# Rows of the quantised FFN's scales by way of DRAM, in pieces of 8 bytes

## The chip, the cores and the metric

The kernel runs on one core of a Trainium2 chip. The metric is device time in microseconds of one execution, lower is better. Before the change three runs took 2035.65, 2041.41 and 2042.34 us, median 2041.41. A core has five engines that run side by side[...]: PE (TensorE, matrix products, with PEld for its weight loads), DVE (VectorE), ACT (ScalarE), POOL (GpSimd) and SP (SyncE, which only issues DMAs here). They wait for one another by semaphores.

## What is computed

Two decoder layers over x of 32 batches x 128 tokens x 256 features: attention, cross-attention and a feed-forward network (FFN) in each. Only the last part, layer 1's FFN, is touched. It quantises its activations twice, once before each product, with one scale per token:

```python
def act_quant(x):
    scale = 127.0 / jnp.clip(jnp.max(jnp.abs(x), axis=-1, keepdims=True), 1e-05)
    return jnp.clip(jnp.round(x * scale), -128, 127) / scale
...
h = bit_linear(x, w1)                       # quantised x, ternary w1: 256 -> 1024
h = depthwise_conv1d(h.transpose(0, 2, 1), conv_w, conv_b)   # 3 taps along the tokens
h = h.transpose(0, 2, 1)
h = jax.nn.silu(h)
return bit_linear(h, w2)                    # quantised h, ternary w2: 1024 -> 256
```

A scale belongs to a token. The kernel has h with features on the 128 partitions and tokens along the free axis, so that the convolution runs along the free axis. To multiply by a token's scale there, a row of 256 token scales must stand on every partition.

## The kernel before

**Stages.** Attention and cross-attention of layer 0 (to about 430 us), layer 0's mixture of experts (to about 1300 us), and `layer1`, which holds the rest. x stays in SBUF throughout, in tiles of four batches.

**Units.** `layer1` splits the 32 batches into NU = 16 units of U = 2 batches, so T = 256 tokens. `unit(u)` returns small functions ("pieces"), one per step: names in d_ are the mixer's, m_ the MLP's, e_ the cross-attention's, f_ the quantised FFN's. The table `PLAN` gives each piece a round, from 0 to 89, and unit u starts STEP = 11 rounds after unit u-1, so some eight units are in work at once. The loop at the end of `layer1` walks the rounds and calls the pieces; that is the program's order.

**Order on the engines.** The products go through `mm` and the transposes through `turned` (L206, L209), which keep PE's instructions in program order. On DVE, ACT, POOL and SP the tile framework orders the instructions itself, from the program's order and its own estimate of when operands are ready. [...] 

**The FFN's steps.** `f_norm` (round 55) normalises x, takes the largest magnitude of each token (`am`, L1259) and calls `scales`, which makes the scale (`qs`, L1010) and its inverse times the weight's mean (`dq`, L1012), both [128 tokens, 2 batches]. `f_quant` scales and rounds (L1265, L1267). `f_flip` (58) transposes the rounded x and calls `on_rows` for dq. `f_h` (60 to 64) makes the first product in four chunks of 256 features and multiplies each by dq's rows (`d`, L1277); `f_z` and `f_taps` are the convolution (L1282, L1292, L1296, L1298), `f_silu` the activation (L1305), `f_top` and `f_am` (67 to 75) the largest magnitude of each token (L1311, L1316, L1323) and its scales. `f_rows` (78) calls `on_rows` for qs; `f_round` (79, 81) multiplies the four chunks of z by qs's rows (L1332) and rounds them (L1333); `f_out` (89) is the second product, its scaling by dq (L1346) and the store (L1349).

**`on_rows` before.** For each of the unit's batches it broadcasts one column of scales along the free axis and multiplies by the identity, so that every partition gets the same row; ACT copies the result from PSUM to SBUF (L1021). It is called twice per unit, once with dq and once with qs.

Other work named later: `m_y`, `m_fc` and `m_out` (tiles y_m, f_m, sT_m, m_m) are the MLP; `e_s`, `e_exp`, `e_soft` and `e_at` (s_e, nm_e, at_e, lv_e) the cross-attention's softmax, with exp on ACT (L1217); `d_v` makes u_d on POOL (L1091); `d_q2` needs a logarithm on ACT (L1097); `d_stats`, `d_nb` (st_d, rs_d, nb_d, ms_d) are the next unit's layer norm. ACT reloads its function table when it changes between exp, logarithm and silu. The loads of `kv_e` and the stores of `out` are layer 1's only other DMAs by SP.

Of the kernel before, what the change touches and what calls it, by code (L numbers as in the profile page):

```python
# [10 lines left out]
F32 = mybir.dt.float32  # L11
# [3 lines left out]
ALU = mybir.AluOpType  # L15
AX = mybir.AxisListType

P = 128
S = 128
# [56 lines left out]
def decoder(ctx: ExitStack, tc: tile.TileContext, a: dict, out: bass.AP):  # L76
    nc = tc.nc
    V, A, PE, GP = nc.vector, nc.scalar, nc.tensor, nc.gpsimd
# [8 lines left out]
    dram = ctx.enter_context(tc.tile_pool(name="scratch", bufs=1, space=bass.MemoryType.DRAM))  # L87
    psp = ctx.enter_context(tc.tile_pool(name="ps", bufs=8, space=bass.MemoryType.PSUM))

    def bank(name, dt=F32):  # L90
        return psp.tile([P, 512 if dt == F32 else 1024], dt, tag="ps", name=name)
# [22 lines left out]
    def con(name):  # L114
        at, w = C_AT[name]
        return cst[:, at : at + w]

    ident, blk, pm = con("ident"), con("blk"), con("pm")
# [86 lines left out]
    def mm(out, lhsT, rhs, start, stop):  # L205
        tc.keep_in_program_order(PE.matmul(out, lhsT=lhsT, rhs=rhs, start=start, stop=stop))  # L206

    def turned(out, in_, by=None):
        tc.keep_in_program_order(PE.transpose(out, in_, ident if by is None else by))  # L209
# [12 lines left out]
    U = 2  # L222
    T = U * S
    NU = NB // U
    ckv = dram.tile([NU, P, 2, U * D], F32, name="ckv")
    rw = keepc.tile([P, 2, NB], F32, name="rw")
    slots = keepc.tile([P, 2, NB], I32, name="slots")
    wm = keepc.tile([P, 2], F32, name="wm")
# [683 lines left out]
    def layer1(wd):  # L912
# [4 lines left out]
        w1 = wq[:, 0, :].rearrange("p (c h) -> p c h", c=2)  # L917
# [3 lines left out]
        with tc.tile_pool(name="pl", bufs=1) as pool, tc.tile_pool(name="pl1", bufs=1) as keep:  # L921
# [10 lines left out]
            def sb(tag, name, bufs=1, dt=F32, shape=(2, T)):  # L932
                return pool.tile([P, *shape], dt, tag=tag, name=name, bufs=bufs)

            def flat(t):
                return t.rearrange("p a b -> p (a b)")

            def bank3(name, n=T):
                return bank(name)[:, : 2 * n].rearrange("p (a b) -> p a b", a=2)

            def sm(tag, name, w=U, bufs=3):
                return small.tile([P, w], F32, tag=f"l_{tag}", name=f"{tag}_{name}", bufs=bufs)
# [34 lines left out]
            def flipped(src, dst, n, dt=F32):  # L977

                pt = bank(f"pt_{n}", dt)[:, : 2 * T]
                for c in range(2):  # L980
                    for i in range(U):
                        turned(
                            pt[:, c * T + i * S : c * T + (i + 1) * S], src[:, i, c * P : (c + 1) * P],
                            ident if dt == F32 else ident_b,
                        )
                A.copy(flat(dst), pt)
                return dst

            def halves(w, m, xT, name):

                p = bank3(name)
                for e in range(2):
                    for c in range(2):
                        mm(p[:, e, :], w[:, c, (m + e) * P : (m + e + 1) * P], xT[:, c, :], c == 0, c == 1)
                return p
# [9 lines left out]
            def scales(am, k, name):  # L1005

                V.tensor_scalar(am, am, 1e-5, None, ALU.max)
                s = sm(f"qs{k}", name)
                V.reciprocal(s, am)
                V.tensor_scalar(s, s, 127.0, None, ALU.mult)  # L1010
                dq = sm(f"dq{k}", name)
                V.tensor_scalar(dq, am, 1.0 / 127.0, wm[:, k : k + 1], ALU.mult, ALU.mult)  # L1012
                return s, dq

            def on_rows(v, k, name):

                p = bank(name)[:, :T]
                for i in range(U):
                    mm(p[:, i * S : (i + 1) * S], v[:, i : i + 1].to_broadcast([P, P]), ident, True, True)
                r = pool.tile([P, T], F32, tag=f"rows{k}", name=f"{name}_sb", bufs=2)  # L1020
                A.copy(r, p)  # L1021
                return r[:, None, :].to_broadcast([P, 2, T])

            def unit(u):
                x = X[u * U // G][:, u * U % G : u * U % G + U, :]
                d_, m_, e_, f_ = f"d{u}", f"m{u}", f"e{u}", f"f{u}"
                o = {}
# [223 lines left out]
                def f_norm():  # L1251
                    o["xf"] = xn = sb("xf", f"xn_{f_}")
                    for i in range(U):
                        V.tensor_scalar(
                            xn[:, i, :], x[:, i, :], o["mv"][:, i, 0:1], o["rs"][:, i : i + 1],
                            ALU.subtract, ALU.mult,
                        )
                    am = sm("am", f_)
                    V.tensor_reduce(am, xn, AX.X, ALU.max, apply_absolute_value=True)  # L1259
                    o["s1"], o["dq1"] = scales(am, 0, f_)  # L1260

                def f_quant():
                    xn = o["xf"]
                    for i in range(U):
                        V.tensor_scalar(xn[:, i, :], xn[:, i, :], o["s1"][:, i : i + 1], MAGIC, ALU.mult, ALU.add)  # L1265
                    o["xi"] = sb("xi", f"xi_{f_}", 2, BF16)
                    V.tensor_scalar(flat(o["xi"]), flat(xn), MAGIC, 127.0, ALU.subtract, ALU.min)  # L1267

                def f_flip():
                    o["hT"] = flipped(o["xi"], sb("xTf", f"xT_{f_}", 2, BF16), f_, BF16)  # L1270
                    o["rows1"] = on_rows(o["dq1"], 1, f"rows1_{f_}")

                def f_h(k):
                    if k == 0:
                        o["z"] = sb("z", f"z_{f_}", 3, shape=(NHC, T))
                    o["d", k] = sb("d", f"d_{f_}_{k}", 4)
                    V.tensor_tensor(o["d", k], halves(w1, 2 * k, o["hT"], f"h_{f_}_{k}"), o["rows1"], ALU.mult)  # L1277

                def f_z(k):
                    for j in range(2):  # L1280
# [37 lines left out]
                def f_am():  # L1318
                    pt = bank3(f"am_{f_}", S)
                    for i in range(U):  # L1320
                        turned(pt[:, i, :], o["top"][:, 0, i * S : (i + 1) * S])
                    am = sm("am2", f_)
                    V.tensor_reduce(am, pt, AX.X, ALU.max)  # L1323
                    o["s2"], o["dq2"] = scales(am, 1, f_)

                def f_rows():
                    o["rows2"] = on_rows(o["s2"], 2, f"rows2_{f_}")
                    o["zi"] = sb("zi", f"zi_{f_}", 2, BF16, (NHC, T))

                def f_round(k):  # L1330
                    z = o["z"][:, 2 * k : 2 * k + 2, :]
                    V.tensor_tensor(z, z, o["rows2"], ALU.mult)  # L1332
                    V.tensor_scalar(  # L1333
                        flat(o["zi"][:, 2 * k : 2 * k + 2, :]), flat(z), MAGIC, MAGIC, ALU.add, ALU.subtract
                    )
# [16 lines left out]
                for k in range(4):  # L1352
                    for of in (gather, m_fc, m_out, f_h, f_z, f_taps, f_silu, f_top, f_round):
                        pieces[f"{of.__name__}{k}"] = partial(of, k)
                return pieces

            units = [unit(u) for u in range(NU)]
            pieces = {r: names.split() for r, names in PLAN}
            for t in range(STEP * (NU - 1) + PLAN[-1][0] + 1):
# [92 lines left out]
def program(arrays):  # L1452
    import concourse.bacc as bacc

    nc = bacc.Bacc("TRN2", target_bir_lowering=False, num_devices=1)
    args = {
        k: nc.dram_tensor(f"in_{k}", v.shape, mybir.dt.from_np(v.dtype), kind="ExternalInput").ap()
        for k, v in arrays.items()
    }
    out = nc.dram_tensor("out", arrays["x"].shape, F32, kind="ExternalOutput").ap()  # L1460
    with tile.TileContext(nc) as tc:
        decoder(tc, args, out)
    return nc
# [9 lines left out]
```

## Time and profile before

| | us |
|---|---|
| median of three runs | 2041.41 |
| the profiled execution | 2041.52 |
| its span (first to last instruction) | 2039.4 |
| PE busy in the span | 1807.9 (89%) |
| DVE busy | 1166.9 (57%) |
| ACT busy | 1080.8 (53%) |
| POOL busy | 421.9 (21%) |

The span in 40 equal slices of 51 us, each digit the busy share in tenths, PEclk the clock that PE was granted:

```profile
PE   6999999899986799999999995379989999999863
DVE  6877667787777512101111111454677888888787
ACT  4454548888885422222222221235677777777662
POOL 4100000000000111111111102852333333333221
PEclk8999999998998899999999998689999999999976
DMA  4000010111002845555546553310000000000000
```

Layer 1 is the part from the 26th slice on. A share over the whole span says little about one stage: DVE is idle through the experts and four fifths busy in layer 1. Below, line numbers are those of this profile, "x4" behind a row is the number of instructions merged in it, and the duration of a single PE row reaches a little beyond the start of the next[...].

### The profile page before, as it was taken

What the parts mean: (1) busy time and instruction counts of PE and PEld (TensorE: products, weight loads), DVE (VectorE), ACT (ScalarE), POOL (GpSimd) and SP (SyncE); (2) the same over time, 40 slices, a digit from 0 to 9 for tenths busy, and PEclk for the clock granted to TensorE, in tenths of its full rate; (3) what the DMA queues carried; (4) which work ended last, traced back from release to release, by engine and by line L of the source; (5) the groups of instructions that cost most, each with busy time, mean ns of one, the idle gap of its engine ahead of it and who ended that gap; (6) DMA issues with size and microseconds to landing.
All of it is one profiled execution on the core that took longest, in us unless ns stands there. A gap on an engine that the chain in (4) does not pass through costs nothing.

```text
span 2039.4 us, 35437 instructions
## 1 busy us (share of the span) xinstructions
PE 1807.9 (89%) x13432; PEld 1477.4 (72%) x13432; DVE 1166.9 (57%) x3716; ACT 1080.8 (53%) x2584; POOL 421.9 (21%) x445
## 2 busy tenths in 40 slices
PE   6999999899986799999999995379989999999863
PEld 4777766676665478888888885268878887888752
DVE  6877667787777512101111111454677888888787
ACT  4454548888885422222222221235677777777662
POOL 4100000000000111111111102852333333333221
PEclk8999999998998899999999998689999999999976
DMA  4000010111002845555546553310000000000000
GB/s 155 3 2 3 8 38 22 33 33 52 16 19 75 325 174 180 202 192 187 211 173 210 183 189 120 87 49 11 11 11 27 16 17 21 27 16 21 27 11 21
DMA packets 51517, 162.13 MB, mean 79 GB/s; under 512 B 5392, under 2 KB 32144, under 8 KB 46224
## 3 DMA queue, kind: packets, MB, share of 16 engines
q1 hardware_dynamic: 44816, 141.99, 19.6%
q0 software_dynamic: 6528, 17.83, 3.1%
q8 instruction: 108, 1.77, 0.4%
q14 instruction: 65, 0.53, 0.1%
HBM read 132.80 MB, written 27.00 MB: 78 GB/s over the span
## 4 chain that ended last, share of the span: by engine, by line
PE 51%; DVE 26%; ACT 10%; POOL 6%; issue 4%; DMA 3%; SPq 0%; POOLq 0%; DVEq 0%; ACTq 0%
PE h L206 12%; PE y L206 12%; ACT sd_b L531 4%; PE od_a L206 3%; DVE top_f L1311 3%; DVE sd_b L518 2%; POOL z_f L1298 2%; PE st_a L206 2%; PE m_m L206 2%; PE et_b L209 2%; PE f_m L206 1%; DMA yr<-ys,slots 1%; DVE rd_a L497 1%; DVE nm L444 1%; PE q_a L206 1%
## 5 line engine op out<-in xcount | busy, mean ns | idle before, releaser
L820 ACT ACTIVATE hTs<-h,moe 128x256 f32<-128x256 f32 x288 | 136.3, 473 | 374.5 <-PE h L206 374.5
L206 PE MATMUL h<-xTs,moe 128*128 128x256 f32 x1152 | 254.7, 379 | 1.0 <-issue 1.0
L206 PE MATMUL y<-moe,hTs 128*128 128x256 f32 x1152 | 254.6, 379 | 0.0
L206 PEld LDWEIGHTS h<-xTs,moe 128*128 128x128 f32 x1152 | 218.7, 190 | 30.9 <-issue 1.2
L206 PEld LDWEIGHTS y<-moe,hTs 128*128 128x128 f32 x1152 | 216.2, 190 | 27.9
L531 ACT ACTIVATE sd_b<-sd_b,nan_b 128x128 f32<-128x128 f32 x512 | 173.8, 387 | 28.9 <-DVE nan_b L525 28.7
L795 POOL DMA_INDIRECT xr<-xs,who x72 | 68.3, 948 | 469.6 <-PE xs L209 426.8
L808 DVE COPY xTs<-xs 128x512 f32<-128x512 f32 x36 | 24.9, 690 | 236.1 <-PE xs L209 236.1
L832 DVE TENSOR_TENSOR yt<-y,moe 128x256 f32<-128x256 f32 x72 | 30.5, 424 | 215.7 <-PE y L206 215.7
L206 PE MATMUL m_m<-wd,sT_m 128*128 128x256 f32 x512 | 119.4, 381 | 0.0
L206 PE MATMUL f_m<-hT_m,wd 128*128 128x256 f32 x512 | 116.9, 383 | 0.0
L518 DVE CUSTOM_DVE_ANT_0 sd_b<-nd_b,s_b 128x128 f32<-128x128 f32 x512 | 113.0, 278 | 5.4 <-PE s_b L206 5.4
L1298 POOL TENSOR_TENSOR z_f<-z_f,e_f 128x508 f32<-128x508 f32 x64 | 70.7, 1104 | 197.3 <-ACT e_f L1296 110.1
L206 PEld LDWEIGHTS f_m<-hT_m,wd 128*128 128x128 f32 x512 | 96.4, 193 | 12.9 <-issue 0.5
L206 PEld LDWEIGHTS m_m<-wd,sT_m 128*128 128x128 f32 x512 | 95.8, 192 | 12.6 <-ACT sT_m L1158 0.2
L497 DVE RECIPROCAL rd_a<-od_a 128x256 f32<-128x256 f32 x32 | 56.0, 1751 | 63.2 <-PE od_a L206 63.2
L1282 ACT ACTIVATE z_f<-d_f,pv 128x256 f32<-128x256 f32 x128 | 70.3, 590 | 35.7 <-DVE d_f L1277 35.6
L544 POOL COPY dens_b<-den_b 128x256 f32<-128x256 f32 x32 | 12.8, 399 | 363.6 <-DVE den_b L542 202.3
L1292 DVE SCALAR_TENSOR_TENSOR z_f<-d_f,pv,z_f 128x254 f32<-128x254 f32 x128 | 64.1, 509 | 37.6 <-ACT z_f L1282 36.7
L474 ACT ACTIVATE et_a<-st_a 128x512 f32<-128x512 f32 x128 | 66.4, 614 | 27.6 <-PE st_a L206 27.6
L444 DVE TENSOR_REDUCE nm<-s_a 128x4 f32<-128x512 f32 x128 | 79.0, 680 | 2.6 <-PE s_a L206 2.6
L206 PE MATMUL s_b<-kEO_b,qT_b 32*128 32x256 f32 x512 | 53.3, 435 | 22.9 <-ACT kEO_b L313 17.0
(358 smaller groups left out, 4007.2 us busy)
## 6 DMA issues: line engine op xcount, KB each, us to landing
moe<-in_moe SPq DMA_DIRECT2D x36, 2180.0 KB, 8.6
ys<-yt SPq DMA_DIRECT2D x36, 256.0 KB, 2.3
ckv<-kv SPq DMA_DIRECT2D x8, 1024.0 KB, 5.2
kv_e<-ckv SPq DMA_DIRECT2D x16, 512.0 KB, 3.6
x<-in_x SPq DMA_DIRECT2D x8, 512.0 KB, 8.8
cT_b<-in_ctxT SPq DMA_DIRECT2D x8, 512.0 KB, 3.8
xs<-xn_c SPq DMA_DIRECT2D x8, 512.0 KB, 3.0
cT_k<-in_ctxT SPq DMA_DIRECT2D x8, 512.0 KB, 7.1
```

Source lines behind the costliest of these rows:

```text
L206: tc.keep_in_program_order(PE.matmul(out, lhsT=lhsT, rhs=rhs, start=start, stop=stop))
L444: V.tensor_reduce(nms[i % 2][:, at : at + 2 * (P - HD)].rearrange("p (e x) -> p x e", e=2)[:, :2, :], sp[r], AX.X, ALU.max, negate=True,)
L474: A.activation(et[:, r].rearrange("p j q -> p (j q)"), st[r], AF.Exp)
L497: V.reciprocal(rd, od[:, 2 * S :])
L518: V.tensor_tensor_reduce(sd[:, r, j, :], nd[:, i, :], sp[r][:, j, :], SLOPES[head(r, j)], -3e38, ALU.add, ALU.max, mx[:, 4 * r + j : 4 * r ...
L531: A.activation(sd[:, r, j, :], sd[:, r, j, :], AF.Exp, bias=nan[:, 4 * r + j : 4 * r + j + 1], accum_out=den[:, h : h + 1] if r % 2 else None,
L795: GP.indirect_dma_start(out=xr[h], out_offset=None, in_=xs[:, :], in_offset=bass.IndirectOffsetOnAxis(ap=who[:, q : q + 1], axis=0),)
L820: A.activation(hT[:, hc, :], p[:, :TS], AF.Relu, bias=b1[:, hc : hc + 1])
L1282: A.activation(o["z"][:, hc, :], o["d", k][:, j, :], AF.Identity, scale=cw[:, hc, 1:2], bias=cb[:, hc : hc + 1],)
L1292: V.scalar_tensor_tensor(z[:, :, 1:], d[:, j, :].rearrange("p (b t) -> p b t", b=U)[:, :, : S - 1], cw[:, hc, 0:1], z[:, :, 1:], ALU.mult, ...
L1298: GP.tensor_tensor(z[:, :, : S - 1], z[:, :, : S - 1], e.rearrange("p h (b t) -> p (h b) t", b=U)[:, :, 1:], ALU.add,)
L1311: V.tensor_reduce(o["top"][:, k, :], o["z"][:, 4 * k : 4 * k + 4, :].rearrange("p h t -> p t h"), AX.X, ALU.max, apply_absolute_value=True,)
```

## The change

For units 0 to 13, `on_rows` no longer uses PE and ACT. It writes the [128, 2] scales of a unit to a DRAM buffer `aside`, one piece of 8 bytes (two batches) from each partition, and reads the resulting 256 numbers back with a broadcast to all 128 partitions. SP issues both DMAs. The call moves to where the scale is made: for dq from `f_flip` to `f_norm`, for qs from `f_rows` to `f_am`. `PLAN` is untouched. Units 14 and 15 keep the products and the copy, at their old places.

In DRAM the two batches of a token lie side by side, so a row read back is ordered token by token, with the batches alternating. The multiplications by the rows (L1277 and L1332) therefore read their second operand with a step of two numbers; both are written with a four-dimensional view (`by_batch`), in all 16 units.

```diff
+    aside = dram.tile([NU, 2, S, U], F32, name="aside")
...
-            def on_rows(v, k, name):
-
-                p = bank(name)[:, :T]
-                for i in range(U):
-                    mm(p[:, i * S : (i + 1) * S], v[:, i : i + 1].to_broadcast([P, P]), ident, True, True)
-                r = pool.tile([P, T], F32, tag=f"rows{k}", name=f"{name}_sb", bufs=2)
-                A.copy(r, p)
-                return r[:, None, :].to_broadcast([P, 2, T])
+            def by_dram(u):
+                return u < NU - 2
+
+            def on_rows(v, k, u):
+                r = pool.tile([P, T], F32, tag=f"rows{k}", name=f"rows{k}_f{u}", bufs=2)
+                if by_dram(u):
+                    nc.sync.dma_start(out=aside[u, k - 1], in_=v)
+                    nc.sync.dma_start(
+                        out=r, in_=aside[u, k - 1].rearrange("s i -> (s i)").partition_broadcast(P)
+                    )
+                    r = r.rearrange("p (s i) -> p i s", i=U)
+                else:
+                    p = bank(f"rows{k}_p{u}")[:, :T]
+                    for i in range(U):
+                        mm(p[:, i * S : (i + 1) * S], v[:, i : i + 1].to_broadcast([P, P]), ident, True, True)
+                    A.copy(r, p)
+                    r = r.rearrange("p (i s) -> p i s", i=U)
+                return r[:, None, :, :].to_broadcast([P, 2, U, S])
+
+            def by_batch(t):
+                return t.rearrange("p a (i s) -> p a i s", i=U)
...
                     o["s1"], o["dq1"] = scales(am, 0, f_)
+                    if by_dram(u):
+                        o["rows1"] = on_rows(o["dq1"], 1, u)
...
                     o["hT"] = flipped(o["xi"], sb("xTf", f"xT_{f_}", 2, BF16), f_, BF16)
-                    o["rows1"] = on_rows(o["dq1"], 1, f"rows1_{f_}")
+                    if not by_dram(u):
+                        o["rows1"] = on_rows(o["dq1"], 1, u)
...
-                    V.tensor_tensor(o["d", k], halves(w1, 2 * k, o["hT"], f"h_{f_}_{k}"), o["rows1"], ALU.mult)
+                    V.tensor_tensor(
+                        by_batch(o["d", k]), by_batch(halves(w1, 2 * k, o["hT"], f"h_{f_}_{k}")), o["rows1"], ALU.mult
+                    )
...
                     o["s2"], o["dq2"] = scales(am, 1, f_)
+                    if by_dram(u):
+                        o["rows2"] = on_rows(o["s2"], 2, u)
...
                 def f_rows():
-                    o["rows2"] = on_rows(o["s2"], 2, f"rows2_{f_}")
+                    if not by_dram(u):
+                        o["rows2"] = on_rows(o["s2"], 2, u)
...
-                    V.tensor_tensor(z, z, o["rows2"], ALU.mult)
+                    V.tensor_tensor(by_batch(z), by_batch(z), o["rows2"], ALU.mult)
```

## The prediction

> **What bounds the kernel now.** First the stage table (busy time per engine in stretches). The change touches only the last third, layer 1, so I cut that into periods, one per unit of two batches:
>
> ```profile
> core 0: us, PE busy (x) PEld busy (x) DVE busy (x) ACT busy (x) POOL busy (x), PEclk, DMA share, GB/s
> ...
> 1595.20:1635.24 40.04, 38.18 (x208) 32.47 (x207) 33.65 (x89) 29.57 (x57) 15.19 (x14) 1.00 0.07 20
> ```
>
> The columns are length, then busy us of each engine. A unit takes 40.04 us from about 1555 to 1875 (eight periods): PE is busy 38.18 of it at a granted clock of 1.00, VectorE 33.65, DMA 7%. So PE is nearly the bound, with 1.86 us idle. The waits of PE over these eight periods say where:
>
> ```profile
> PE h_f L206 <- ACT xT_f L986: 4.9, 8, 0.7
> PE at_e L209 <- ACT sT_m L1158: 4.6, 5, 0.9
> PE q_d L206 <- ACT hT_d L986: 2.8, 8, 0.4
> PE at_e L209 <- DVE at_e L1225: 2.2, 3, 0.7
> ```
>
> Total us, times, longest. Per period: 0.61 for xT_f, 0.85 for at_e (both of its rows), 0.35 for hT_d; together 1.81, all the idle time. All three wait for work that is late on ScalarE or VectorE. After 1875 the pipeline drains, PE is busy 105 of 164 us, and VectorE (129 of 164) and latencies decide.
>
> **What goes.** PE's timeline in one period:
>
> ```profile
> 1716.69 0.61 PE L206 MATMUL rows_f<-cst,qs_f 128*128 128x128 f32 x4
> 1717.14 1.06 PE L206 MATMUL s_e<-kv_e,k_e 128*128 128x128 f32 x8
> ...
> 1720.85 0.66 PE L206 MATMUL rows_f<-cst,dq_f 128*128 128x128 f32 x4
> 1721.35 0.60 PE L209 MATMUL pt_e<-cst,xn_e 128*128 128x128 f32 x4
> ```
>
> From start to start, the rows of qs take 0.45 us of PE's queue and those of dq 0.50, so 0.95 us per unit; in 14 of 16 units 13.3 us leave PE. Two ScalarE copies of 0.37 us (L1021) leave each unit as well, both in the crowded run that ends in xT_f and exp. Two PSUM banks per unit are no longer asked for. In the built order PE keeps everything else in its place.
>
> **What is added: two dependent DMAs for each scale.** SP issues a write of 128 x 8 bytes, waits until it has landed, then issues a 128 KB broadcast read. The near rows, from issue to landing:
>
> ```profile
> kv_e<-ckv SPq DMA_DIRECT2D x16, 512.0 KB, 3.6
> out<-x SPq DMA_DIRECT2D x16, 256.0 KB, 2.1
> ```
>
> Writes to DRAM at this stage land in 2.1 us (4.3 at most). The read is a quarter of kv_e's, so between 2.1 and 3.6; taking part of the difference for bytes I use 2.5. With three semaphore hops of some 0.1 us (small VectorE-to-PE steps in the timeline are of that size) the round trip L is 2.1 + 2.5 + 0.3 = 4.9 us; bounds 4.2 (both at 2.1) and 8.2 (4.3 + 3.6 + 0.3). [...] No row here shows such a write in quiet; it is why my upper bound takes the slowest `out`.
>
> **Where the waits fall.** dq's rows: dq is done at 1714.4 and first used at 1733.6 (d_f, L1277), 19 us for a 5 us trip; free. qs's rows are tighter. The lines of before that bracket it, on VectorE:
>
> ```profile
> 1707.75 0.17 DVE L1010 TENSOR_SCALAR qs_f<-qs_f 128x2 f32<-128x2 f32 x1
> ...
> 1712.47 0.65 DVE L1259 TENSOR_REDUCE am_f<-xn_f 128x2 f32<-128x512 f32 x1
> ...
> 1722.43 1.27 DVE L1332 TENSOR_TENSOR z_f<-z_f,rows_f_sb 128x512 f32<-128x512 f32 x2
> ```
>
> Before, the four multiplications by the rows (L1332) start at 1722.4, because PE gives the rows only at 1716.7. In the built order of the changed kernel they stand directly behind am_f (L1259), that is from 1713.1: qs has 1713.1 - 1707.85 = 5.2 us to come round. At L = 4.9 VectorE does not stall. Queued behind that first multiplication are al_d, xn_f, xi_f (needed by PE's pt_f, spare about 1.8 us), nm_e and so exp, Ln and xT_f on ScalarE.
>
> SP's queue: behind the two waits stand dq's pair, the store of out and the next kv_e. dq comes 6.6 us after qs, when SP is free again; out is waited for by nobody; kv_e is loaded 13 rounds of the plan ahead of s_e, some 47 us (13 x 40.04 / 11). Free, up to L of tens of us.
>
> **What moves.** The four multiplications and two roundings (L1333) go ahead of nm_e, while st_d, the taps of chunk 3 (L1292) and top_f (L1311) go behind it. Up to nm_e VectorE loses about 2.4 + 0.7 of added work and is freed of 1.95 (top_f), 0.87 (taps), st_d and the nb_d/ms_d steps with a 1.07 us ms_d: nm_e comes near 1720.0 instead of 1722.1. Then exp, v_d, the Ln table and xT_f follow on ScalarE, ending near 1724 instead of 1725.8, against a PE that needs it at 1725.4 - 0.95 = 1724.4. The xT_f gap closes. The multiplications also leave the company of u_d on GpSimd, which took 3.50 us beside them (1.28 elsewhere) and made VectorE wait 1.2 us; and at_e is no longer queued behind the top_f maximum (1.40 us there, 0.42 in the median). The at_e gap closes too. hT_d's 0.35 stays. In return VectorE waits for rs_d, now behind chunk 3's add on GpSimd (about 1.8 us idle), and top_f sits between d_f of chunk 0 and chunk 1.
>
> PE alone would then allow 40.04 - 0.95 - 1.46 = 37.6 us. Following the VectorE, ScalarE and GpSimd chain by hand with the durations of the trace (qs, rounds, nm_e, taps, rs_d, u_d, scan, qn_d, pre_d, d_f, top_f, z_f, d_f of chunk 1) I find d_f of chunk 1 about 1.3 us and its z_f about 1.8 us earlier than now: a period near 38.3. I take the slower of the two: **38.3, saving 1.7 us** per steady period.
>
> **The stride.** Pieces of 8 bytes make the multiplications read their second operand with a step of two floats, eight instructions of 512 elements per unit. The nearest strided row is top_f (step 1 KB): 1943 ns for 1024 elements, 1.90 ns each, against 654 ns for 512 in a row (am_f, L1259), 1.28 each. By that row each instruction gains 0.32 us, 2.5 us a period. [...] top_f [...] is not this case, so I take 0; the row's 2.5 stays as a bound.
>
> **Sum.** Eight steady periods x 1.7 = 13.6. The two periods from 1480 to 1555, with rows and not yet everything else: 0.5 each, 1.0. The drain: the last two units are as before; in units 10 to 13 the built order leaves about 5.3 to 7.4 us of other VectorE work behind each scale, so no stall, and PE's two rows_f in the chain of waits at 1915.6 and 1948.8 go (0.96 each), of which I count 1.0. Together 15.6, from the execution's 2041.5 (span 2039.4; the median of the runs is 2041.4): **2026 us**.
>
> **Rivals.** A difference of 0.3% (6 us) is what can be told from none.
> 1. PE alone decides and both gaps close: saving 2.4 x 8, plus ramp and drain 3: 2019. For it: all of PE's idle time is explained by three waits. Against: VectorE's chain has 6 us of waits of its own per period.
> 2. The gain is hidden: the VectorE, ScalarE, GpSimd chain keeps near 40 us, since rs_d, top_f and the moved ScalarE steps eat what PE gives: 2037 to 2041. For it: these engines wait for one another all through the period.
> 3. Slower: the round trip of qs. Above L = 5.2 each us goes onto VectorE; the saving of 1.7 is used up at L = 6.9, and from there nine periods each pay (L - 6.9). At the bound of 8.2 it is 12 us slower, 2053[...]. The stride at its bound (+2.5 - 1.7) would give 2048 without any stall.
> 4. The change doesn't do what it says: excluded by the built order, which has 56 more DMAs and 56 fewer matmuls of rows.
>
> **Chances.** Forecast (2018 to 2035) 0.50; rival 1 (below 2020) 0.13; rival 2, 0.17; rival 3, 0.20. The likeliest case's own range is 2018 to 2036; to leave out no more than two in ten I reach into rival 3 at L near 7.5 and take 2014 to 2047. Faster by over 0.3%: 0.50 + 0.13, less a little that falls within, 0.61; within 0.3%: 0.18; slower: 0.21.
>
> **What would show it.** Right: a period near 38.3 with PE busy 37.2; rows written in about 2 us and read in 2 to 3; no idle before the first z_f multiplication; u_d at 1.28; those multiplications still at 683 ns. Wrong: VectorE idle before that multiplication with the DMA as its releaser (L too small), 0.9 us or more per multiplication (stride), or PE waiting for q_d, h_f or at_e by more than now.

## The result, and the profile after

| | before | changed |
|---|---|---|
| median, us | 2041.24 (4 runs) | 2057.55 (4 runs) |
| span of the profiled execution, us | 2039.4 | 2057.4 |

The changed kernel takes 1.0082 times as long (95% interval 1.0068 to 1.0097): about 16.7 us slower, where 2026 was forecast. The place of the loss is found by cutting both spans at each start of the unit's first scan (L1117 before, L1133 after). Of the 18.0 us between the two spans, 0.9 lie before the first unit with moved rows; 8.0 in the two periods of the ramp, from 1480 on; 8.4 in the eight steady periods (328.95 against 320.58); 0.8 in the drain. Some 1.6 us of the ramp's share go with the granted clock: in its first period it was 0.96 in the profile of before and 0.92 in that of the changed kernel. Of the kernels below that do not stall there, four (only dq, both with the rounds at 82, statistics early) took 39.8 to 39.9 us for that period, at 0.91, and two (rounds at 84, only dq with statistics early) 38.3 and 38.5, at 0.96; before took 38.26.

The stage table of the changed kernel, two steady periods (length, then busy us by engine, granted clock, DMA share and rate):

```profile
core 0: us, PE busy (x) PEld busy (x) DVE busy (x) ACT busy (x) POOL busy (x), PEclk, DMA share, GB/s
1646.00:1687.33 41.33, 37.52 (x202) 31.80 (x201) 33.55 (x89) 28.76 (x55) 13.70 (x13) 1.00 0.14 27
1687.33:1728.46 41.13, 37.04 (x199) 31.31 (x198) 33.55 (x89) 28.74 (x55) 13.71 (x13) 1.00 0.13 27
```

PE is busy about 37.2 us, 1 us less than before: what was to leave PE did leave. But the period is 41.1 on the mean of the eight, not 38.3, and PE idles 4 us of it. (A period given for a run below is the usual one of the first seven; the eighth runs into the drain and differs, 40.65 in before and 41.3 with the rounds at 82.) The waits over eight periods (1564 to 1893; total us, times, longest), on PE and then on VectorE:

```profile
PE q_d L206 <- ACT hT_d L987: 13.0, 8, 1.9
PE h_f L206 <- ACT xT_f L987: 8.9, 7, 1.4
PE at_e L209 <- DVE at_e L1241: 8.5, 8, 1.1
...
DVE z_f L1313 <- ACT z_f L1303: 16.6, 16, 1.6
DVE nb_d L963 <- POOL rs_d L957: 14.8, 8, 1.9
DVE z_f L1356 <- DMA rows_f<-aside: 12.5, 8, 1.9
```

None of the three gaps on PE closed; each grew. The last row is new: in each of the eight units VectorE stands still for the rows of qs, up to 1.9 us. It is the first of the signs of being wrong that the prediction named. VectorE's timeline in one period (start, us, operation, and in brackets the idle time before it and its releaser):

```profile
1718.51 0.17 DVE L1011 TENSOR_SCALAR qs_f<-qs_f 128x2 f32<-128x2 f32 x1
...
1723.23 0.65 DVE L1275 TENSOR_REDUCE am_f<-xn_f 128x2 f32<-128x512 f32 x1
1725.55 0.69 DVE L1356 TENSOR_TENSOR z_f<-z_f,rows_f 128x512 f32<-128x512 f32 x1 [1.67 <-DMA rows_f<-aside]
...
1726.50 0.16 DVE L1008 TENSOR_SCALAR am_f<-am_f 128x2 f32<-128x2 f32 x1
...
1736.75 1.22 DVE L963 SCALAR_TENSOR_TENSOR nb_d<-mv_d,rs_d 128x2 f32<-128x2 f32 x1 [1.85 <-POOL rs_d L957]
...
1740.38 1.24 DVE L1241 TENSOR_SCALAR at_e<-at_e,den_e 128x128 f32<-128x128 f32 x2
```

qs is done at 1718.68 and am_f at 1723.88: the slack is the 5.2 us of the forecast. The rows can be used at 1725.55, 6.87 us after qs (6.7 to 7.1 in the steady units). What is queued behind waits with them: L1008 needs nothing but am_f, and starts 2.62 us after am_f's end, where in the kernel before (L1007) it starts 0.58 us after it, at 1713.70. SP's queue (start of the issue, us) splits that:

```profile
1718.70 0.32 SPq L1024 DMA_DIRECT2D aside<-qs_f  x1
1721.41 0.32 SPq L1025 DMA_DIRECT2D rows_f<-aside  x1
```

From the write's issue to the read's 2.7 us, from there to the use 4.1. The DMA list, medians from issue to landing, says the same:

```profile
rows_f<-aside SPq DMA_DIRECT2D x28, 128.0 KB, 4.0
...
aside<-dq_f SPq DMA_DIRECT2D x14, 1.0 KB, 2.9
aside<-qs_f SPq DMA_DIRECT2D x14, 1.0 KB, 2.9
```

### The profile page after: what moved, and what is told of

Read it like the earlier page. It is cut to its first block, busy times and chain, and to the rows that moved or that the text cites. A ratio compares the mean times of both kernels' runs of the same rounds, so it can differ in the third digit from the quotient of the medians.

```text
span 2057.4 us, 35298 instructions
## 1 busy us (share of the span) xinstructions
PE 1795.3 (87%) x13320; PEld 1463.5 (71%) x13320; DVE 1164.4 (57%) x3716; ACT 1070.6 (52%) x2556; POOL 416.2 (20%) x445
## 4 chain that ended last, share of the span: by engine, by line
PE 51%; DVE 24%; ACT 8%; DMA 7%; issue 5%; POOL 5%; SPq 0%; POOLq 0%; DVEq 0%; ACTq 0%
PE h L206 12%; PE y L206 12%; ACT sd_b L532 4%; PE od_a L206 3%; DMA rows_f<-aside 3%; DVE sd_b L519 2%; DMA aside<-qs_f 2%; DVE top_f L1332 2%; DVE z_f L1356 2%; PE st_a L206 2%; POOL z_f L1319 2%; DMA yr<-ys,slots 2%; PE f_m L206 2%; DVE z_f L1313 2%; PE et_b L209 2%
## 5 line engine op out<-in xcount | busy, mean ns | idle before, releaser
L206 PEld LDWEIGHTS h<-xTs,moe 128*128 128x128 f32 x1152 | 218.7, 190 | 30.9 <-issue 1.2
L532 ACT ACTIVATE sd_b<-sd_b,nan_b 128x128 f32<-128x128 f32 x512 | 173.8, 388 | 28.6 <-DVE nan_b L526 28.4
```

Of the source, the lines that this page charges most:

```text
L532: A.activation(sd[:, r, j, :], sd[:, r, j, :], AF.Exp, bias=nan[:, 4 * r + j : 4 * r + j + 1], accum_out=den[:, h : h + 1] if r % 2 else None,
```

## The experiments

Theory A of the expectations is that the round trip of qs is longer than its slack, and that VectorE's stall for it makes the loss; its rivals, as they are named there, look elsewhere, above all to the new order on VectorE. Each ratio is to runs of the kernel before that stood beside it (medians 2039.9 to 2040.9). First each half of the change by itself, and the use of qs's rows at three later rounds of `PLAN`.

**Only dq by DRAM.** qs keeps the products and its old round.

```diff
-            def by_dram(u):
-                return u < NU - 2
+            def by_dram(u, k=1):
+                return u < NU - 2 and k == 1
```

> Only dq's rows go by DRAM (units 0 to 13); qs's rows are made by products as before. Theory A (all of the loss comes from VectorE waiting for qs's round trip of 7.0 us and from the order that puts its multiplications early): no stall is left, 0.50 us of PE per unit goes, so some 5 us faster than before, 2036 (2031 to 2041). Rival B (the DMAs themselves cost: SP's queue, DMA traffic): about half of the 17 us loss, 2049. The first d_f multiplication should wait for no DMA.

Measured 2036.38, ratio 0.9979 (0.9972 to 0.9986); period 39.3 to 39.5. Faster than before by 4 us: this half of the change is a gain.

**Only qs by DRAM** (`k == 2` in the same place).

> Only qs's rows go by DRAM; dq's rows are made by products as before. Theory A: the whole loss stands, and the 0.50 us of PE per unit from dq are not saved: 2057 to 2064, with VectorE idle about 1.7 us per unit before the first z_f multiplication. Rival B: about half of the loss, 2049.

Measured 2060.79, ratio 1.0101 (1.0082 to 1.0120); period 41.8 to 42.1. The whole loss, and more, is in this half. The stall is longer here than in the changed kernel, 1.9 to 2.4 us in each unit.

**Changed kernel, rounds later.**

```diff
-        (79, "f_round0 f_round1 f_round2"), (81, "f_round3"), (89, "f_out"),
+        (82, "f_round0 f_round1 f_round2"), (84, "f_round3"), (89, "f_out"),
```

> The changed kernel with f_round0 to f_round2 at round 82 and f_round3 at 84 in the plan (79 and 81 before): the built order puts st_d and its rs_d ahead of the multiplications, and about 5 us more work between qs and the first of them. Theory A: no idle time before the multiplication and none at nb_d, a period of 38.3 to 39 us instead of 41.1, so 2026 to 2034. Rival B: the plan changes little, 2050 to 2058. Rival C (the place of the multiplications ahead of nm_e costs by itself, not the round trip): half gone, 2040 to 2048, since three of four still stand ahead of nm_e.

Measured 2034.46, ratio 0.9969 (0.9959 to 0.9978); period 38.9. That is just outside the 2026 to 2034 of theory A, with the period that it named. It is faster than before and than the changed kernel, and has the lowest median of the study, but its interval overlaps that of dq alone (0.9972 to 0.9986). VectorE's waits, eight periods:

```profile
DVE z_f L1313 <- ACT z_f L1303: 18.8, 16, 1.7
DVE pre_d L1146 <- POOL pre_d L1143: 11.1, 8, 1.4
DVE xn_f L1270 <- POOL rs_f L957: 3.0, 8, 0.5
DVE z_f L1356 <- DMA rows_f<-aside: 0.9, 1, 0.9
```

The stall is gone but for one, and the wait of nb_d is gone too. In its timeline the first multiplication now comes 9 us after qs:

```profile
1705.55 0.17 DVE L1011 TENSOR_SCALAR qs_f<-qs_f 128x2 f32<-128x2 f32 x1
...
1714.69 1.28 DVE L1356 TENSOR_TENSOR z_f<-z_f,rows_f 128x512 f32<-128x512 f32 x2
```

**The same at 84 and 86.**

> The changed kernel with f_round0 to f_round2 at round 84 and f_round3 at 86: the built order has two of the four multiplications ahead of nm_e and nb_d ahead of all of them, near the order of the kernel before. Theory A: 2026 to 2034, as with round 82. Rival B: 2050 to 2058. Rival C: clearly better than with round 82, by 4 us or more.

Measured 2040.92, ratio 1.0009 (0.9997 to 1.0021): a miss. VectorE doesn't stall for the rows, yet the period is 40.25 to 40.6. GpSimd's u_d takes 2.46 us on the mean here (1.27 in the changed kernel) and VectorE waits for it in all eight units. Near 1724 it stands beside the top_f maximum and the last multiplication by qs's rows again, as it stood beside multiplications before the change; that these make it slow was not tried. The period is 40.6 where the granted clock was 0.96 and 40.25 where it was 1.00.

**At 81 and 83.**

> The changed kernel with f_round at 81 and 83, one round earlier than the run that gained. The built order keeps the first two multiplications where the change put them, directly behind am_f, so the slack for the round trip of qs stays at 5.2 us; only the fourth moves behind nb_d. Theory A: the stall of 1.5 to 2 us per unit stays, a period of 40.3 to 41.2, 2048 to 2058. If the slack were not the point, moving by two rounds of the three needed should bring two thirds of the gain, 2042.

Measured 2056.87, ratio 1.0077 (1.0060 to 1.0094). In this kernel nb_d's wait shrinks to 4.7 us over eight periods (14.8 in the changed kernel), the DMA's grows to 17.6 (14.2 over the same stretch), and the period stays at 41.2 to 41.6. So taking 1.3 us of nb_d's wait out of each unit did not shorten it; what that wait costs at most is worked out below.

**The new order with products.** The kernel before, with `f_rows` one round earlier. Its rows leave PE at 1712.5, and its VectorE order is nearly the change's, without a DMA. Three things differ: the second half of st_d stands ahead of the first multiplication, GpSimd's rs_d ahead of chunk 3's add, and GpSimd's u_d behind the next small step, rs_d12i, where the changed kernel has it ahead.

```diff
-        (71, "f_taps3"), (72, "f_silu3"), (73, "f_top1"), (75, "f_am"), (78, "f_rows"),
+        (71, "f_taps3"), (72, "f_silu3"), (73, "f_top1"), (75, "f_am"), (77, "f_rows"),
```

> The kernel before, with f_rows at round 77 instead of 78 in the plan: qs's rows are still made by products, but the built order on VectorE is now that of the changed kernel, the first multiplication directly behind am_f, nm_e behind all four, st_d's statistics and nb_d behind nm_e. So this is the change's order without its DMAs (and with PE's 0.95 us still there). Theory A (stall and order add up): the 1.7 us stall is missing, the wait at nb_d stays: a period of 39.5 to 40.5 us, 2036 to 2046. Rival C (the order alone carries the loss): a period of 41 or more, 2050 or later. Rival D (the stall alone does, the order is free): 38.5 to 39.3, 2026 to 2034.

Measured 2043.18, ratio 1.0015 (1.0006 to 1.0023); period 40.45. This order costs a little, 0.4 us a period, where the forecast had the order gain. VectorE's waits:

```profile
DVE u_d L1122 <- POOL u_d L1091: 17.0, 8, 2.1
...
DVE nb_d L962 <- POOL rs_d L956: 4.7, 8, 0.6
```

The first row is this kernel's own: in the changed kernel and with only qs by DRAM VectorE does not wait for u_d. GpSimd's timelines, first here, then in the changed kernel:

```profile
1726.04 0.71 POOL L956 TENSOR_TENSOR rs_d12i<-ve_d12i,mhalf 128x2 f32<-128x2 f32 x1 [0.63 <-DVE ve_d12i L954]
1726.71 1.27 POOL L1091 TENSOR_TENSOR u_d<-u_d,v_d 128x512 f32<-128x512 f32 x1
...
1736.69 1.27 POOL L1107 TENSOR_TENSOR u_d<-u_d,v_d 128x512 f32<-128x512 f32 x1
1738.59 1.00 POOL L957 TENSOR_TENSOR rs_d12i<-ve_d12i,mhalf 128x2 f32<-128x2 f32 x1 [0.63 <-DVE ve_d12i L955]
```

So the run shows that an order much like the change's, without a stall, is far from losing 17 us; it does not weigh the changed kernel's own order.

**The next unit's statistics ahead of the rounds.** The changed kernel, with `d_stats` three rounds earlier; the rounds stay at 79 and 81.

```diff
-        (0, "gather0 gather1"), (1, "gather2 gather3"), (3, "added"), (4, "d_stats"), (5, "d_nb"),
+        (0, "gather0 gather1 gather2 gather3"), (1, "added d_stats"), (5, "d_nb"),
```

> The changed kernel with only the next unit's added and d_stats moved from rounds 3 and 4 to round 1; f_round stays at 79. In the built order the statistics and ve_d then stand ahead of the multiplications, which come behind xi_f, about 4 us later than in the changed kernel. Theory A: no stall (slack about 9 us against 7.0), rs_d asked for early, a period near 38.9 as with round 82: 2031 to 2037. If what made round 82 fast was something else in its plan, it stays above 2045.

Measured 2036.84, ratio 0.9982 (0.9973 to 0.9991); period 38.7 to 39.0. The first multiplication comes 8.7 to 9.0 us after qs, and one stall of 1.2 us is left. This edit, like the one to round 82, gives slack and puts the statistics back in front at once, so it agrees with A but can't weigh the two.

**Two controls.** The rounds at 82 in the kernel before, and the statistics early with only dq by DRAM:

> A control for round 82: the kernel before, products as they were, with f_round at 82 and 84. The built order on VectorE hardly differs from before. If round 82 alone makes the gain that the changed kernel showed with it, this is near 2034 too; if the gain needs the rows to come without PE (theory A), this is 2038 to 2043, a period of 40.

> A candidate for a version that beats both: dq's rows by DRAM, qs's by products, and the next unit's statistics at round 1. Built order as with dq alone but for d_f of chunk 0, which comes before the ga product. Theory A: no stall, PE the bound with 0.50 us less per unit; as with dq alone or a little better, 2033 to 2037.

Measured 2039.39, ratio 0.9997 (0.9988 to 1.0006), period 40.05; and 2035.89, ratio 0.9976 (0.9967 to 0.9985), period 39.3 to 39.5. Without DMAs for qs neither move of the plan does anything that can be told from none. Round 82 therefore helps the changed kernel by what it does to qs's DMAs and the work behind them, not by itself. Against before, most of the 6 us at 82 is dq's half, 4 us by itself.

**What the round trip is made of.** The kernel before, with further DMAs in units 0 to 13 for which nobody waits, one kind per unit in turn: the same pair of write and broadcast read (pw, prf_f); a broadcast read of a row of an input (pro_f); a read of 128 different pieces of 1 KB (prd_f); a write of 128 pieces of 512 bytes (pz). One run, 2041.90 us.

```diff
+                    if kind == 0:
+                        nc.sync.dma_start(out=p8[u], in_=o["s2"])
...
+                        nc.sync.dma_start(out=r, in_=p8[u].rearrange("s i -> (s i)").partition_broadcast(P))
+                    elif kind == 1:
...
+                        nc.sync.dma_start(out=r, in_=a["rv"][:T].partition_broadcast(P))
+                    elif kind == 2:
...
+                        nc.sync.dma_start(out=r, in_=ckv[0][:, 0, :T])
+                    else:
+                        nc.sync.dma_start(out=p512[u], in_=o["z"][:, 6, :128])
```

> The kernel before with one or two extra DMAs per unit that nobody waits for, to measure the disputed costs by themselves: a write of 128 pieces of 8 bytes and a broadcast read of what it wrote; a broadcast read of 1 KB that has lain in DRAM from the start; a read of 128 different pieces of 1 KB; a write of 128 pieces of 512 bytes. If small pieces make the write slow, 8-byte pieces land clearly later than 512-byte ones (2.1 us by the stores of out); if reading one address 128 times makes the read slow, both broadcasts take about 4 us and the 128 different pieces about 2.5; if it is the freshness of the bytes, the old row reads in about 2.5 and the fresh one in 4.

The DMA list (count, KB each, median us from issue to landing):

```profile
prf_f<-pw SPq DMA_DIRECT2D x4, 128.0 KB, 3.9
pro_f<-in_rv SPq DMA_DIRECT2D x4, 128.0 KB, 2.9
prd_f<-ckv SPq DMA_DIRECT2D x3, 128.0 KB, 2.1
pz<-z_f SPq DMA_DIRECT2D x3, 64.0 KB, 1.5
pw<-qs_f SPq DMA_DIRECT2D x4, 1.0 KB, 3.0
```

128 pieces of 8 bytes land in 3.0 us, twice the time of 128 pieces of 512 bytes. The read of 128 KB takes 2.1 us from 128 places and 2.9 from one row; the two also lie in different buffers, a scratch one and an input. From the row written by the kernel it takes 3.9, so the three lie between the outcomes that were set out. The four reads behind that median differ: 4.1 and 4.4 us where the read was issued within 1 us of the write's landing, 3.4 and 3.6 where SP issued it some 12 us later. So of the last 1.0 a part came with the short distance from the write, in two reads against two; the rest, 0.5 to 0.7, is not settled.

**All of them on one ruler.** One period of each kernel near 1710, counted in us from the end of qs, to the start of four steps on VectorE: the first multiplication by qs's rows, nm_e, the step that needs GpSimd's u_d, and the multiplication by dq's rows of chunk 1 (d_f); then the length of that period.

| kernel | first z_f x rows | nm_e | u_d | d_f, chunk 1 | period |
|---|---|---|---|---|---|
| before | 14.5 | 14.2 | 19.2 | 29.6 | 40.1 |
| products at 77 | 5.9 | 12.5 | 18.7 | 30.0 | 40.5 |
| only qs by DRAM | 7.6 | 14.6 | 20.4 | 31.7 | 42.1 |
| changed | 6.9 | 13.9 | 19.7 | 30.9 | 41.4 |
| only dq by DRAM | 14.5 | 14.2 | 19.2 | 28.4 | 39.5 |
| rounds at 82 | 9.0 | 12.2 | 17.0 | 28.6 | 39.1 |

From d_f of chunk 1 to the next qs it is 10.5 us in each row but one (11.1 with only dq by DRAM), and 10.2 in the other periods of the changed kernel. So the periods come to differ before that d_f. PE still waits in all of these kernels, least with the rounds at 82 (9.6 us in eight periods).

**What a stall costs.** The stall varies from unit to unit. For each of eight units, from its qs to the next (the table's ruler), take the stall from the length:

| kernel | stall, us | qs to qs, us | difference, us |
|---|---|---|---|
| only qs by DRAM | 1.93 to 2.39 | 41.68 to 42.14 | 39.75 to 39.78 |
| rounds at 81 | 2.00 to 2.38 | 41.19 to 41.58 | 39.19 to 39.22 |
| changed | 1.53 to 2.21 | 40.96 to 41.65 | 39.43 to 39.47, once 39.73 |
| before | none | 39.84 to 40.10 | |
| only dq by DRAM | none | 39.29 to 39.50 | |

Each microsecond of stall lengthens its unit by a full microsecond, whether the granted clock was 1.00 or 0.96 (with only qs it was 0.96 in four of eight periods). What is left without it, an estimate for a kernel whose rows come in time, is 39.45 in the changed kernel, 0.5 less than the mean of before (39.97) and about that of only dq (39.37); with only qs it is 39.75, 0.2 less than before. So the loss in the steady periods is the stall, 1.77 us a unit on the mean, less a gain of 0.5 that dq's half alone also gives. The order on VectorE costs nothing that can be seen here, and gains next to nothing. The same difference in the rounds at 81, 39.2, bounds nb_d's wait: 1.3 us less of it goes with 0.25 us less of period.

The ramp's two periods pay more: their stalls are 1.9 and 2.2 us, and they are 5.3 us longer than those of rounds at 82, which has the same granted clock in the second and 0.91 against 0.92 in the first.

## Why the prediction was wrong

**What held.** PE lost its 0.95 us per unit. dq's rows are free: one wait of 1.7 us for them in the whole run, and that half alone gains. The stride costs nothing (684 ns for a multiplication, 683 before), so the 0 that was taken stands (an estimate of the author's, that no row of before showed), and the 2.5 us of the strided row falls. GpSimd's u_d came down to 1.27 us from 3.5 in five of the eight periods and 1.28 in three. SP's queue delayed nobody: behind the experts PE, VectorE, ScalarE and GpSimd wait for no DMA but the rows (19.7 us, all on VectorE), and in the steady period above each write is issued within 0.1 us of its scale's end. The drain moved by 0.8 us. The slack of qs, 5.2 us, was read rightly from the built order, and so was what waits behind it: rival 3 names the mechanism that happened, and its "each us goes onto VectorE" is what the stalls show.

**First step that failed: the round trip, "2.1 + 2.5 + 0.3 = 4.9 us".** Measured 6.9: about 2.7 for the write with its hop and 4.1 for the read with its own. Both terms were taken from rows of another shape. `out` is a large store in pieces of 1 KB; in the probe 128 pieces of 8 bytes took 3.0 us, twice the 1.5 of 128 pieces of 512. The read was scaled by bytes from `kv_e`, which reads different places; in the probe the same bytes from one row took 0.8 us more, from a row that the kernel wrote 1.8 more. Why the small pieces land later and the one row reads later, no run shows. The upper bound of 8.2 held the value, and the trip should have been taken from nearer to it, because no row was near in shape. With L = 6.9 against 5.2 us of room, 1.7 us of VectorE's time is gone each period, and all of it arrives in the period.

**Second step that failed: "a period near 38.3", the chain followed by hand.** Even with L = 6.9 rival 3's own sum gives no change (38.3 + 1.7 = 40.0), and the steady period is 1.1 above that. Without its stall the changed kernel would gain about 0.5 us a period and not 1.7. In the period of the tables, with the stall of 1.67 taken off, the first part came as forecast: nm_e is 2.0 us earlier than before (2.1 forecast), and VectorE waits 1.85 us for rs_d (1.8 forecast). But d_f of chunk 1 is only 0.35 us earlier, where 1.3 was forecast. What is missing lies in steps that lengthen beside GpSimd. The forecast took the 1.40 us of the top_f maximum beside GpSimd's qn_d back to 0.42. It did fall to 0.42, but at_e now stands beside qn_d (1739.56 to 1741.35) and takes 1.24 for its two instructions, where it took 0.47 in this period of before. (In three of the eight periods of before the two already had it the other way round, at_e 1.48 and the maximum 0.40.) In the same way nb_d grew from 0.15 to 1.22 beside GpSimd's u_d, but ms_d fell from 1.07 to 0.16 and gives nearly all of that back. The net, some 0.8 and 0.2 us, is about the 0.95 that is missing; the last 0.2 lies behind d_f. This is an estimate: the chain was not written down step by step, and no run gave the changed kernel's at_e its old length. The rows of before:

```profile
1717.43 0.15 DVE L962 SCALAR_TENSOR_TENSOR nb_d<-mv_d,rs_d 128x2 f32<-128x2 f32 x1
...
1717.68 1.07 DVE L1055 TENSOR_TENSOR ms_d<-ms_d,mv_d 128x2 f32<-128x2 f32 x1
...
1729.21 1.40 DVE L1316 TENSOR_TENSOR top_f<-top_f 128x256 f32<-128x256 f32 x1
1730.54 0.47 DVE L1225 TENSOR_SCALAR at_e<-at_e,den_e 128x128 f32<-128x128 f32 x2
```

**What this does to "the xT_f gap closes" and "the at_e gap closes".** In the changed kernel the stall delays nm_e and at_e, and both gaps grew. With the rounds at 82, the rows have 9 us, the statistics end (ve_d) 7.0 us after qs instead of 16.2, and of PE's waits only the one for hT_d is left. But "hT_d's 0.35 stays" failed in both: 13.0 us in eight periods in the changed kernel, 9.6 with the rounds at 82, 2.8 before. With the rounds at 82 the period is 38.9: near the forecast's 38.3, in a kernel that the change isn't.

**The range.** It ended at 2047, at L near 7.5 with the hand-made period of 38.3. The two errors, 1.7 us of stall and some 1.2 of chain in each steady period, had the same sign, and the range did not let them run together.

## What to carry to other kernels

Before a value goes by way of DRAM, compare the whole trip, write, wait and broadcast read (6.7 to 7.6 us in the kernels here), with the distance from its maker to its first user in the queue of the engine that will wait; take the landing times from transfers of the same piece size and the same pattern of addresses (here 3.0 us for pieces of 8 bytes against 1.5 for 512, and 2.9 for one row against 2.1 for 128 places). Look at the user's place when the maker's changes: the same DMAs lost 16 us with 5.2 us of room and gained 6 with 9, of which 4 is the half that had 19 us of room from the start. To weigh a stall that varies from unit to unit, take it from each unit's length: if the rest is constant, the stall is paid whole, and the rest is what the kernel would do without it. And when a chain is added up from the durations of a trace, allow for steps that lengthen in new company: the lengthening here moved from one step to its neighbour (the top_f maximum from 1.40 to 0.42 us, at_e from 0.47 to 1.24).

## What the hardware showed unasked

- Fewer bytes did not make a shorter DMA: 1 KB in 128 pieces of 8 bytes took 3.0 us, 64 KB in 128 pieces of 512 bytes 1.5.
- 128 KB read from one DRAM row took longer than from 128 different places, 2.9 against 2.1 us (an input against a scratch buffer, so the buffer may have a share), and a row written by the kernel longer again: 4.1 and 4.4 us within 1 us of the write's landing, 3.4 and 3.6 some 12 us later.
- Two tiny steps on VectorE that started just behind the start of a GpSimd step lasted until that one ended. nb_d, 128x2, takes 0.15 us in the kernel before and 1.22 in the changed kernel, where it runs from 1736.75 to 1737.97 and GpSimd's u_d from 1736.69 to 1737.96. In the kernel before, ms_d does the same beside chunk 3's add (1717.68 to 1718.75, and 1717.65 to 1718.74).
- Each load of ScalarE's function table took 1.28 us. From 1300 us on the kernel before has 65 of them, 29 at the softmax's exp (L1217) and 15 at the logarithm (L1097).
